# A four-layer graph network on one core: reciprocals brought to the free axis through HBM scratch tensors

## The chip, the cores and the metric

The kernel runs on one core of one Trainium2 chip. A core has five engines with instruction streams of their own: TensorE (matrix products, PE in the profile; PEld is its weight load), VectorE (DVE), ScalarE (ACT), GpSimd (POOL) and SyncE (SP, which here issues every transfer), and 16 DMA engines that move data between HBM and the on-chip memory SBUF. Matmul results land in PSUM banks. Each engine works its stream in order and waits on semaphores for the others. The metric is device time in microseconds (us), as the median of several runs.

## The reference, cut to what matters

The input is 32 independent graphs of 512 nodes, each with a feature matrix x (512 x 256) and a 0/1 adjacency matrix (512 x 512). Four layers follow; each ends in x = layernorm(x + layer(x)).

```
layer 0   attention with 8 heads, scores masked by adj, softmax over the keys:
          out = (softmax(q k^T / sqrt(32), masked) v) Wo + bo
layer 1   relu(((1+eps) x + adj x) W1 + b1) W2 + b2                 hidden 512
layer 2   h = (eps x + adj x) W1 + b1                               hidden 1024
          h = h * rsqrt(mean(h*h over the 1024) + 1e-6) * weight    (an RMS norm)
          silu(h) W2 + b2
layer 3   softplus of a normalised-Laplacian layer
```

Two factors matter here. In layer 0 each node and head has the reciprocal of its softmax sum. In layer 2 each node has one RMS factor. All is computed in float32.

## The kernel before, in words

A graph's 512 nodes are NT = 4 tiles of 128. Activations that feed a product are kept with the features on the partitions and the nodes on the free axis (qT, kT, oT, hT, aT, gT); those that are normalised per node are kept the other way (y, r1, r2). A factor per node is computed with the nodes on the partitions. Where the tensor that it multiplies has the nodes on the free axis (oT and gT), the factor has to be turned and spread over 128 partitions. That is the place of this change.

**Layer 0.** `attend` (called for two groups of four heads) makes, per node tile, a group of four score products with 32 rows each (sc, L776, row-tiled), then on VectorE mask and row minimum (L800), on ScalarE the exponential with its row sums in rs (L814), on VectorE a block transpose (L850), then a store to HBM (via, four DMAs, L862) and a load (pT, L874) that finish the transposition. The value products (po_att, L893, column-tiled) run over two tiles at once, and their result goes unnormalised to oT. `normalise` (L946) then takes reciprocals of all 32 sums per node (L952), `split` (L910) writes each as three bfloat16 parts, TensorE transposes them (pm_t, L934), a copy brings them to SBUF (mT), and eight small matmuls with a constant selection matrix (pr_r, L963) spread them to the 128 partitions in PSUM. VectorE multiplies oT by that (L974). `pair_sum` with wo (po, L991) follows.

**Layer 2.** Eight products with w21 (pg, L1187) give gT; squares on ScalarE (L1263) are summed on GpSimd into ssq (L549). A transpose (L1270), a reduction (L1273) and one small matmul (pm, L1281) bring the sums to the node axis; VectorE finishes the mean (L1295, L1303), GpSimd takes the power -1/2 (rr). Then `split` again (L917, L924, pm_t, mT), four selection matmuls (pb, L1314), and eight VectorE products of gT by weight and factor (L1326), silu in two halves on ScalarE (L1341) and the product with w22 (po, L991).

**The order.** Nothing is scheduled by a compiler: the function `graph` records every operation of every graph with its reads, writes, engine, estimated cost and stage. The class `Order` then plays through all of them: at each step it takes, on the engine that is free first, the operation with the smallest key. The key is graph number times PERIOD plus the operation's due time, which comes from the operation's earliest and latest time in a lone graph (weighted by LATE) plus an offset per stage (LEAD). So three graphs or so are in flight at once, and attention of one is woven into the later layers of another. The instructions are emitted in that order, and each engine keeps it. TURN_DUE is a penalty for changing between row-, column- and untiled matmuls; HASTE moves the last graph forward. Buffers rotate by tag: four PSUM banks with the tag "m" serve nearly all products, the scores have a set of four banks of their own; adjT has two buffers, gT one.

All DMAs of the program are issued in order by SP. A DMA whose input isn't ready blocks those behind it.

Of the kernel before, what the change touches and what calls it, by code (L numbers as in the profile page):

```python
# [9 lines left out]
F32 = mybir.dt.float32  # L10
BF16 = mybir.dt.bfloat16
AF = mybir.ActivationFunctionType
# [7 lines left out]
RMS_EPS = 1e-6  # L20
HEADS = 8

PERIOD = 65998
LEAD = {
    "adjT": 17900, "agg1": -34100, "agg2": -112800, "degree": 46800, "diag": 80200,
    "lap": -5300, "ln0": -81400, "ln1": -47100, "ln2": 88600, "ln3": -37200, "load": -92700,
    "move": 7000, "pv": 8000, "pz": 22200, "qk": 5800, "rinv": -8800, "rms": -91800,
    "scores": -5600, "silu": 57000, "softplus": -39900, "v": -32400, "w11": -49700,
    "w12": -36000, "w21": 10500, "w22": -22500, "wo": 21900, "x3T": -21500, "xT": 67600,
}  # L30


# [27 lines left out]
class Order:  # L60
# [9 lines left out]
    TABLE, TABLE_DUE = 1300, 9000  # L70

    TURN = {"whole": 93, "row": 290, "col": 150}
    TURN_DUE = 500
    LATE = 0.09
    HASTE = 137

    def __init__(self):
        self.ops = []
# [204 lines left out]
def kernel(  # L283
# [51 lines left out]
    nhalf = const.tile([P, NT], F32, name="nhalf")  # L335
    nc.vector.memset(nhalf, -0.5)

    ident_b = const.tile([P, P], BF16, name="ident_b")
    nc.vector.tensor_copy(ident_b, ident)

    def selector(n, wide, name):

        of = const.tile([P, n], F32, name=f"{name}_of")
        nc.vector.tensor_reduce(
            of, ident[:, 0 : 3 * n].rearrange("p (r x) -> p x r", r=3), axis=AX.X, op=ALU.add
        )
        sel = const.tile([P, n, wide], BF16, name=name)  # L350
        nc.vector.tensor_copy(sel, of.unsqueeze(2).to_broadcast([P, n, wide]))
        return sel

    NX = 2 * NT * HPG
    sel_r = selector(NX, HD, "sel_r")
    sel_t = selector(NT, P, "sel_t")


    id_as = ident.rearrange("p (a s) -> p a s", a=4)
# [148 lines left out]
    def graph(b):  # L508
# [10 lines left out]
        def tmp(shape, tag, bufs, name=None, dtype=F32):  # L519
            return Buf(sb, shape, dtype, tag, f"{name or tag}_{b}", bufs)  # L520

        def pe(cost, fn, r, w, *hold, turn="whole"):

            op([("PE", cost, fn, {"turn": turn})], r, w, hold)

        def dve(cost, fn, r, w, port=False):
            op([("DVE", cost, fn, {"port": 1} if port else {})], r, w)
# [41 lines left out]
        def small(name, bufs=2, shape=None):  # L569
            return Buf(sb, shape or [P, NT], F32, "s_" + name, f"{name}_{b}", bufs)  # L570
# [336 lines left out]
            stage[0] = "rinv"  # L907
            evacuate(lambda: oT[:, g, :], po, [(po,)], [(oT, g)])

        def split(src, n, name):  # L910

            parts = tmp([P, 3, n], "p_" + name, 2, name + "p", dtype=BF16)
            left, left_k = src, []
            for r in range(3):
                dve(
                    190,
                    lambda r=r, left=left: nc.vector.tensor_copy(parts[:, r, :], left()),  # L917
                    [(left,)], [(parts, r)], port=True,
                )
                if r < 2:  # L920
                    rest = small(name + "rest", 2, [P, n])
                    dve(
                        180,
                        lambda r=r, left=left, rest=rest: nc.vector.tensor_tensor(  # L924
                            rest(), left(), parts[:, r, :], ALU.subtract
                        ),
                        [(left,), (parts, r)], [(rest,)], port=True,
                    )
                    left = rest
            pm_t = Buf(ps, [P, P], BF16, "m", f"pm_t_{b}", 4)  # L930
            mT = tmp([P, P], "mT_" + name, 1, dtype=BF16)
            pe(
                65,
                lambda: nc.tensor.transpose(  # L934
                    pm_t[0 : 3 * n, :], parts().rearrange("p r x -> p (r x)"), ident_b
                ),
                [(parts, r) for r in range(3)], [(pm_t,)], mT,
            )
            either(
                [(pm_t,)], [(mT,)],  # L940
                (220, lambda: nc.vector.tensor_copy(mT[0 : 3 * n], pm_t[0 : 3 * n, :])),
                (330, lambda: nc.scalar.copy(mT[0 : 3 * n], pm_t[0 : 3 * n, :])),
            )
            return mT

        def normalise():  # L946

            stage[0] = "rinv"
            rv = small("rv", 2, [P, NX])
            dve(  # L950
                240,
                lambda: nc.vector.reciprocal(rv(), rs().rearrange("p g t j -> p (g t j)")),  # L952
                [(rs, g, t, j) for g in range(2) for t in range(NT) for j in range(HPG)],
                [(rv,)],
            )
            mT = split(rv, NX, "sums")
            for g in range(2):
                pr_r = bank("pr_r")

                def spread(g=g, pr_r=pr_r):  # L960
                    for t in range(NT):
                        x = (g * NT + t) * HPG
                        nc.tensor.matmul(  # L963
                            pr_r[:, t * P : (t + 1) * P],
                            lhsT=sel_r[0 : 3 * NX, x : x + HPG].rearrange("p j e -> p (j e)"),
                            rhs=mT[0 : 3 * NX],
                            start=True,
                            stop=True,
                        )

                pe(240, spread, [(mT,)], [(pr_r,)])
                dve(
                    700,
                    lambda g=g, pr_r=pr_r: nc.vector.tensor_tensor(  # L974
                        oT[:, g, :], pr_r(), oT[:, g, :], ALU.mult
                    ),
                    [(pr_r,)], [(oT, g)],
                )

        def pair_sum(lhs, lhs_k, w, w_k, nk, y, step):  # L980
# [156 lines left out]
        x1 = y  # L1137


        def residual(xin, bias_r, bias_k):  # L1140
            r = tmp([P, NT, D], "y", 3)
            pool(
                2400,
                lambda: nc.gpsimd.tensor_tensor(r(), xin(), rows(bias_r), ALU.add),
                [(xin, t) for t in range(NT)] + [(bias_k,)], [(r, t) for t in range(NT)],
            )
            return r

# [49 lines left out]
        stage[0] = "agg1"  # L1198
        set_diagonal(self1, "self1")
        hT = aggregate(x1)  # L1200
        r1 = residual(x1, b12_r, "b12_r")
        set_diagonal(self2, "self2")
        stage[0] = "w11"
        aT = tmp([P, C1, N], "aT", 1)
# [101 lines left out]
        rr = small("rr")  # L1306
        rsqrt(rr, ms, [(ms,)], [(rr,)])

        mT = split(rr, NT, "rms")
        pb = bank("pb")  # L1310

        def spread_rms():
            for t in range(NT):
                nc.tensor.matmul(  # L1314
                    pb[:, t * P : (t + 1) * P],
                    lhsT=sel_t[0 : 3 * NT, t],
                    rhs=mT[0 : 3 * NT],
                    start=True,
                    stop=True,
                )  # L1320

        pe(240, spread_rms, [(mT,)], [(pb,)])
        for m in range(C2):
            dve(
                750,
# [176 lines left out]
        for rt in row_tiles:  # L1502
# [6 lines left out]
            s_ = lambda part=part: sp[:, part]  # L1509
            z_ = lambda part=part: zy[:, part, 0:D]  # L1510
            x_ = lambda part=part: x3[:, part]
            act(cost, lambda s_=s_, z_=z_: nc.scalar.activation(s_(), z_(), AF.Abs), z0, spk)
            act(
                cost,
                lambda s_=s_: nc.scalar.activation(s_(), s_(), AF.Exp, scale=-1.0), [], spk,
# [75 lines left out]
```

## Time and profile before

| What | Before |
|---|---|
| median of 3 runs | 3356.13 us (3354.51 to 3359.38) |
| profiled execution | 3356.19 us |
| span of its trace | 3354.4 us |
| TensorE busy | 3305.2 us |
| VectorE busy | 2823.6 us |
| ScalarE busy | 1887.3 us |
| GpSimd busy | 843.4 us |
| mean share of the 16 DMA engines | 77%, 677.23 MB moved |
| granted TensorE clock | 0.996 |

The span is the time from the first to the last instruction of the profiled execution; the execution itself is 1.8 us longer. Busy time is the union of an engine's instructions. Consecutive matmuls overlap in the trace, since each record lasts until the result is out, so the price of a matmul is best read from the distance between starts. A float32 product appears as two passes.

### The profile page before, as it was taken

To read this page: it belongs to the slowest core of one execution; us is meant where nothing else is said; L and a number is where in the kernel's file an instruction comes from. 1 tells how busy PE (TensorE), PEld (TensorE's weight loads), DVE (VectorE), ACT (ScalarE), POOL (GpSimd) and SP (SyncE) were. 2 spreads that over 40 slices of the span, in tenths; PEclk is the share of its full clock that TensorE was granted. 3 is DMA by queue.
4 is the path that set the end of the run, shared out by engine and by line. 5 is a ranking of instruction groups with operands and counts; after the bars stand their busy time and mean duration, and the time that the engine had idled before them with its cause. 6 is when DMAs were issued, how large, how long until landed. Compare 5 with 4: busy or idle time off the path is not lost.

```text
span 3354.4 us, 55143 instructions
## 1 busy us (share of the span) xinstructions
PE 3305.2 (99%) x19624; PEld 1980.2 (59%) x19624; DVE 2823.6 (84%) x6412; ACT 1887.3 (56%) x3863; POOL 843.4 (25%) x610
## 2 busy tenths in 40 slices
PE   8999999999999999999999999999999999999997
PEld 5556655566565566565666655665655665556654
DVE  7878888888888888888888888888888888888855
ACT  6555565565655655655555655555656556556533
POOL 1222222322222322222222223222222222232221
PEclk9999999999999999999999999999999999999999
DMA  5878878778878787787787787787887887877820
GB/s 143 246 235 216 207 200 222 226 202 211 204 202 234 204 220 197 206 219 226 201 215 207 202 228 214 208 210 201 215 232 199 214 206 201 225 224 183 206 53 13
DMA packets 768195, 677.23 MB, mean 202 GB/s; under 512 B 540208, under 2 KB 592304, under 8 KB 736176
## 3 DMA queue, kind: packets, MB, share of 16 engines
q1 hardware_dynamic: 767920, 673.71, 76.5%
q8 instruction: 155, 2.54, 0.3%
q14 instruction: 120, 0.98, 0.1%
HBM read 380.52 MB, written 293.08 MB: 201 GB/s over the span
## 4 chain that ended last, share of the span: by engine, by line
PE 96%; DVE 1%; ACT 1%; DMA 1%; issue 0%; POOL 0%; SPq 0%; POOLq 0%; DVEq 0%; ACTq 0%
PE po L991 23%; PE ph L1170 13%; PE pg L1187 13%; PE sc L776 8%; PE po_att L893 7%; PE pz L1436 7%; PE pa_l L1478 7%; PE pa L1187 7%; PE pq L703 6%; PE pv L744 3%; ACT pq L814 0%; PE pr_r L963 0%; PE pb L1314 0%; DVE pq L800 0%; DMA via<-pq 0%
## 5 line engine op out<-in xcount | busy, mean ns | idle before, releaser
L814 ACT ACTIVATE pq<-pq,mx 128x512 f32<-128x512 f32 x1024 | 729.0, 714 | 333.3 <-DVE mx L800 265.7
L800 DVE CUSTOM_DVE_ANT_0 pq<-sc,bias 128x512 f32<-128x512 f32 x1024 | 664.3, 685 | 42.3 <-PE sc L776 23.7
L850 DVE STREAM_TRANSPOSE pq<-pq 128x2048 f32<-128x2048 f32 x248 | 567.9, 2296 | 6.4 <-ACT pq L814 6.4
L1187 PE MATMUL pg<-hT,w 128*128 128x512 f32 x1024 | 480.3, 603 | 2.0 <-DVE gT L1242 2.0
L991 PE MATMUL po<-w,gT 128*128 128x256 f32 x2048 | 451.3, 381 | 6.3 <-ACT gT L1341 6.3
L991 PEld LDWEIGHTS po<-w,gT 128*128 128x128 f32 x2048 | 391.3, 191 | 62.1 <-ACT gT L1341 7.1
L549 POOL TENSOR_TENSOR ssq<-ssq,sq 128x512 f32<-128x512 f32 x217 | 276.9, 1276 | 521.6 <-ACT sq L1263 521.2
L1187 PEld LDWEIGHTS pg<-hT,w 128*128 128x128 f32 x1024 | 184.6, 190 | 251.0 <-issue 238.1
L776 PE MATMUL sc<-kT,qT 32*128 32x512 f32 x2048 | 291.9, 640 | 3.0 <-DVE mx L800 3.0
L893 PEld LDWEIGHTS po_att<-pT,v 128*32 128x32 f32 x8192 | 216.3, 110 | 99.1 <-issue 49.2
L893 PE MATMUL po_att<-pT,v 128*32 128x128 f32 x8192 | 251.2, 275 | 5.5 <-DMA pT<-via 5.5
L1478 PE MATMUL pa_l<-zy,adjT 128*128 128x256 f32 x1024 | 243.0, 385 | 0.0
L1044 POOL TENSOR_TENSOR rstd<-ve,nhalf 128x4 f32<-128x4 f32 (+1 forms) x132 | 135.6, 1028 | 422.5 <-DVE ve L1039 417.5
L1242 DVE TENSOR_SCALAR gT<-pg,b_c 128x512 f32<-128x512 f32 x187 | 140.3, 751 | 120.0 <-PE pg L1187 119.9
L549 POOL TENSOR_TENSOR sp<-sp,y 128x1024 f32<-128x1024 f32 x31 | 73.4, 2367 | 657.7 <-ACT sp L1528 644.7
L1436 PE MATMUL pz<-wsn,xnT 128*128 128x512 f32 x512 | 236.9, 606 | 0.7 <-ACT sq L1263 0.6
L1170 PE MATMUL ph<-adjT,y 128*128 128x512 f32 x512 | 227.0, 596 | 4.7 <-ACT y L1070 4.7
L1170 PE MATMUL ph<-adjT,y_att 128*128 128x512 f32 x512 | 228.2, 598 | 0.0
L1187 PE MATMUL pa<-hT,w 128*128 128x512 f32 x512 | 228.1, 598 | 0.0
L991 PE MATMUL po<-w,aT 128*128 128x256 f32 x1024 | 226.5, 379 | 0.0
L991 PEld LDWEIGHTS po<-w,aT 128*128 128x128 f32 x1024 | 194.3, 190 | 28.0 <-ACT aT L1218 0.8
L1478 PEld LDWEIGHTS pa_l<-zy,adjT 128*128 128x128 f32 x1024 | 189.3, 190 | 29.9 <-issue 0.7
(165 smaller groups left out, 4896.3 us busy)
## 6 DMA issues: line engine op xcount, KB each, us to landing
via<-pq SPq DMA_DIRECT2D x992, 256.0 KB, 4.4
pT<-via SPq DMA_DIRECT2D x248, 1024.0 KB, 6.4
adj<-in_adj_dram SPq DMA_DIRECT2D x32, 1024.0 KB, 7.9
adjT<-in_adj_dram SPq DMA_DIRECT2D x124, 256.0 KB, 6.0
x<-in_x_dram SPq DMA_DIRECT2D x32, 512.0 KB, 6.1
xT<-in_x_dram SPq DMA_DIRECT2D x124, 128.0 KB, 5.9
x3d<-y SPq DMA_DIRECT2D x31, 512.0 KB, 3.9
xnT<-x3d SPq DMA_DIRECT2D x124, 128.0 KB, 3.7
```

The costliest lines, as they stand in the source:

```text
L549: lambda: nc.gpsimd.tensor_tensor(dst(), dst(), src(), ALU.add), {},
L703: nc.tensor.matmul(pq(), lhsT=w[:, c, m * P : (m + 1) * P], rhs=xT[:, c, :], start=(c == 0), stop=(c == DC - 1),)
L776: nc.tensor.matmul(sc[:, j, :], lhsT=qT[hp, g, t * P : (t + 1) * P], rhs=kT[hp, g, :], start=True, stop=True,)
L800: lambda t=t, j=j, sc=sc, row=row: nc.vector.tensor_tensor_reduce(out=row(), in0=sc[:, j, :].rearrange("p (a n) -> p a n", a=4), in1=bias[ ...
L814: lambda t=t, j=j, row=row: nc.scalar.activation(row(), row(), AF.Exp, bias=mx[:, t, j : j + 1], scale=-1.0, accum_out=rs[:, g, t, j : j + 1],
L850: lambda pq=pq: nc.vector.transpose(pq().rearrange("p a j c s -> p (a j c s)"), pq().rearrange("p a j c s -> p (a j c s)"),),
L893: nc.tensor.matmul(po[j * HD : (j + 1) * HD, t * P : (t + 1) * P], lhsT=v[:, c, h * HD : (h + 1) * HD], rhs=pT[:, :, j, c, :], start=(c == 0),
L991: nc.tensor.matmul(po[:, i * D : (i + 1) * D], lhsT=lhs[:, k, t * P : (t + 1) * P], rhs=w[:, k, :], start=(i == 0 and k == 0), stop=(i == ...
L1170: nc.tensor.matmul(ph(), lhsT=xin[:, m, c * P : (c + 1) * P], rhs=adjT[:, m, :], start=(m == 0), stop=(m == NT - 1),)
L1187: nc.tensor.matmul(pa(), lhsT=w[:, c, m * P : (m + 1) * P], rhs=hT[:, c, :], start=(c == 0), stop=(c == DC - 1),)
L1436: nc.tensor.matmul(pz(), lhsT=xnT[:, c, t * P : (t + 1) * P], rhs=wsn[:, c, :], start=(c == 0), stop=(c == DC - 1),)
L1478: nc.tensor.matmul(pa[:, i * D : (i + 1) * D], lhsT=adjT[:, m, t * P : (t + 1) * P], rhs=zy[:, m, D : 2 * D], start=(m == 0), stop=(m == N ...
```

## The change

The turning by TensorE is replaced, in both places, by a round trip through scratch tensors in HBM, with a read that repeats a row over partitions.

In `normalise`, VectorE takes the reciprocals and transposes the 128 x 32 tile in 32 x 32 blocks. Four DMAs store the blocks in rd, which then holds one row of 128 nodes for each tile and head; four DMAs read the rows back, each repeated over the 32 partitions of its head, to the SBUF tensor of. VectorE multiplies oT by of.

In layer 2, one DMA stores the 512 factors, element by element, as a row of HBM (rrd), and one reads this row into all 128 partitions (pb, which is now an SBUF tensor with the tag of the squares). `split`, its casts and transposes, the selection matmuls and their constants go.

The planner's constants are new: PERIOD, all 28 LEAD offsets, TURN_DUE, LATE and HASTE. So the order of all operations differs between the two kernels. Two operations also get a dependency that only the planner sees: the residual of layer 1 of graph b comes after the first softplus operation of graph b-2.

```diff
-PERIOD = 65998
+PERIOD = 62758
 LEAD = {
-    "adjT": 17900, "agg1": -34100, "agg2": -112800, "degree": 46800, "diag": 80200,
...
+    "adjT": 30100, "agg1": -27200, "agg2": -109700, "degree": 60800, "diag": 115000,
...
-    TURN_DUE = 500
-    LATE = 0.09
-    HASTE = 137
+    TURN_DUE = 1750
+    LATE = 0.50
+    HASTE = 2161
...
-        def split(src, n, name):
...
         def normalise():
             rv = small("rv", 2, [P, NX])
+            def turned():
+                nc.vector.reciprocal(rv(), rs().rearrange("p g t j -> p (g t j)"))
+                nc.vector.transpose(rv(), rv())
...
-            mT = split(rv, NX, "sums")
+            rd = Buf(dr, [NX, P], F32, "rd", f"rd_{b}", 2)
+            of = tmp([P, 2, NT, P], "of", 1)
+            def away():
+                for i in range(4):
+                    nc.sync.dma_start(
+                        rd[:, 32 * i : 32 * i + 32], rv[32 * i : 32 * i + 32, :]
+                    )
+            def back():
+                v = rd().rearrange("(gt j) q -> j gt q", j=HPG)
+                for j in range(HPG):
+                    nc.sync.dma_start(
+                        of[j * HD : (j + 1) * HD].rearrange("p g t q -> p (g t) q"),
+                        v[j].partition_broadcast(HD),
+                    )
...
-                pe(240, spread, [(mT,)], [(pr_r,)])
                 dve(
                     700,
-                    lambda g=g, pr_r=pr_r: nc.vector.tensor_tensor(
-                        oT[:, g, :], pr_r(), oT[:, g, :], ALU.mult
-                    ),
-                    [(pr_r,)], [(oT, g)],
+                    lambda g=g: nc.vector.tensor_tensor(
+                        oT[:, g, :], of[:, g].rearrange("p t q -> p (t q)"), oT[:, g, :], ALU.mult
+                    ),
+                    [(of,)], [(oT, g)], port=True,
                 )
...
-        mT = split(rr, NT, "rms")
-        pb = bank("pb")
...
-        pe(240, spread_rms, [(mT,)], [(pb,)])
+        rrd = Buf(dr, [NT, P], F32, "rrd", f"rrd_{b}", 2)
+        pb = tmp([P, N], "sq", 2, "pb")
+        def rr_away():
+            with nc.allow_non_contiguous_dma(reason="one factor per node"):
+                nc.sync.dma_start(rrd().rearrange("t p -> p t"), rr())
+        op([("SP", 3000, rr_away, {"issue": 560, "lat": 300})], [(rr,)], [(rrd,)])
+        op(
+            [(
+                "SP", 4500,
+                lambda: nc.sync.dma_start(
+                    pb(), rrd().rearrange("t p -> (t p)").partition_broadcast(P)
+                ),
+                {"issue": 560, "lat": 300},
+            )],
+            [(rrd,)], [(pb,)],
+        )
```

## The prediction

> **What bounds the kernel now.** I read the page first: busy time and the chain that ended last. Then TensorE's waits, busy time by stretch, and TensorE's timeline in one graph.
>
> ```profile
> span 3354.4 us, 55143 instructions
> PE 3305.2 (99%) x19624; PEld 1980.2 (59%) x19624; DVE 2823.6 (84%) x6412; ACT 1887.3 (56%) x3863; POOL 843.4 (25%) x610
> PE 96%; DVE 1%; ACT 1%; DMA 1%; issue 0%; POOL 0%; SPq 0%; POOLq 0%; DVEq 0%; ACTq 0%
> ```
>
> The second answer, for a stretch in the middle (second number: TensorE's busy time, fourth: VectorE's):
>
> ```profile
> core 0: us, PE busy (x) PEld busy (x) DVE busy (x) ACT busy (x) POOL busy (x), PEclk, DMA share, GB/s
> 1000.00:2000.00 1000.00, 1000.00 (x5980) 593.91 (x5979) 862.14 (x1956) 570.65 (x1178) 263.94 (x189) 1.00 0.80 213
> ```
>
> TensorE never idles there. A busy matmul could still be a slow one, so I looked at starts. The one-column matmul pm comes at 1586.08 and next at 1688.21: 102.13 us a graph, the same to 0.01 us over 28 graphs in a row. TensorE's waits list nothing between 300 and 3150 us; the 30 us that it does wait lie in the first and last graphs. So in 28 of 32 graphs the time is TensorE's instruction list, and I price that list by starts, since durations overlap:
>
> ```profile
> 1586.08 0.29 PE L1281 MATMUL pm<-red,quad 128*128 128x16 f32 x2
> 1586.22 1.96 PE L1436 MATMUL pz<-wsn,xnT 128*128 128x512 f32 x4
> 1588.11 1.14 PE L776 MATMUL sc<-kT,qT 32*128 32x512 f32 x8
> ...
> 1590.15 1.89 PE L1478 MATMUL pa_l<-zy,adjT 128*128 128x256 f32 x8
> 1591.97 0.22 PE L934 MATMUL pm_t<-ident_b,rmsp 128*12 128x128 bf16 x1
> 1592.12 1.99 PE L1478 MATMUL pa_l<-zy,adjT 128*128 128x256 f32 x8
> 1594.05 0.39 PE L1314 MATMUL pb<-mT_rms,sel_t 12*128 12x128 bf16 x4
> 1594.37 3.72 PE L1478 MATMUL pa_l<-zy,adjT 128*128 128x256 f32 x16
> 1598.02 1.14 PE L776 MATMUL sc<-kT,qT 32*128 32x512 f32 x8
> ...
> 1601.79 13.98 PE L991 MATMUL po<-w,gT 128*128 128x256 f32 x64
> 1615.69 1.14 PE L776 MATMUL sc<-kT,qT 32*128 32x512 f32 x8
> ```
>
> ```profile
> 1655.85 1.88 PE L703 MATMUL pq<-xT,wk 128*128 128x512 f32 x4
> 1657.57 0.22 PE L934 MATMUL pm_t<-ident_b,sumsp 128*96 128x128 bf16 x1
> 1657.62 1.94 PE L1187 MATMUL pg<-hT,w 128*128 128x512 f32 x4
> 1659.39 0.61 PE L963 MATMUL pr_r<-mT_sums,sel_r 96*128 96x128 bf16 x8
> 1659.94 1.14 PE L776 MATMUL sc<-kT,qT 32*128 32x512 f32 x8
> ```
>
> A pass of 512 columns takes (1657.57-1655.85)/4 = 0.43 us, one of 256 about 13.90/64 = 0.216. Before a row-tiled group (sc) about 0.09 us are lost, after it 0.10.
>
> **What the Trainium skill says.** (1) "TensorEngine Tiling (Array Packing)", Key Properties: a change of tiling mode drains TensorE. The trace agrees, and shows it for the narrow matmuls pm_t (12 columns of weights) and pb (12 rows) too. (2) The Trainium skill, "DMA: Bandwidth & Descriptors", "Anatomy of one DMA" (written for another issuing path): a fixed part of some 2 us, mostly the receipt of the write. The trace's smallest medians to landing are 3.0 to 3.9 us, so I use the trace. (3) The Trainium skill, "SBUF — State Buffer", "SBUF: two separate sides": a VectorE operation with two SBUF inputs and a GpSimd one exclude each other. Agrees: L1152 (two SBUF inputs) takes 654/693/1936 ns min/median/max, L974 with one input from PSUM 677/683/693.
>
> **The change, part by part.**
> *TensorE, sums.* One pm_t, 0.05; eight pr_r, 0.55 less the 0.09 that any matmul would lose ahead of sc: 0.46. Together 0.51 x 32 = 16.3 us.
> *TensorE, RMS.* pa_l, pm_t and pb stand from 1590.15 to 1598.02 = 7.87; 32 passes of 0.216 are 6.91, and 0.09 ahead of sc stays: 0.87 goes. In the 30 graphs with this pattern 26.1 us.
> *Moved order.* Constants of the planner change with it (PERIOD, LEAD and three more), so TensorE's whole order is new. In the built order pm stands right ahead of an sc group in 29 graphs, where a drain is paid anyway; now it costs 0.14 and (1.89-4x0.43-0.09) = 0.08 after it, of which I take 0.17 off: 4.9 us. Visits to row or column mode fall from 295 to 289, 6 x 0.2 = 1.2 us. All other matmuls are the same in number.
> Sum 48.5 us: the period becomes about 100.6.
> *VectorE* loses ten small casts and subtractions and two copies, 66 us in all by its groups, and gains 32 transposes of 128x32. It had 16% idle: nothing by itself. The two oT products and eight gT products now have both inputs in SBUF. GpSimd has nothing queued during the gT products; oT products stand between its ssq additions and can lose one of them (1.28 us), with over 5 us to the next sc.
> *DMA.* Per graph 10 more issues on SP's queue (56 before), 4 of 4 KB, 4 of 128 KB, one of 2 KB in 4-byte elements and one of 256 KB. SP's issues in the trace run 0.3 to 0.7 us: 3 to 7 us of 102, on a queue that spends most of its time waiting. About 0.8 MB on top of 21 MB.
> *Sums' round trip.* The reciprocals are ready when the last exponential is; the second po_att evacuation comes more than 30 us later in the built order, and the wo product later still. Two transfers of some 4 us, with via and pT issues between, are covered.
> *RMS round trip*, the tight one. Between ms and the first gT product VectorE's built order holds four half-statistics (2x0.53), four zy (0.67), four score tiles (0.61), a transposition (2.22) and one y_att (0.60): 9.0 us, stretched to 9.8 by the pz passes it follows. The power on GpSimd takes 1.1 of it: 8.7 remain for both transfers. Not shown in the trace: a store of 512 4-byte elements and a read of one row into 128 partitions. Nearest rows: xnT (1024 runs of 128 B) 3.7, x3d 3.9, via 4.4; the column loads at the start 3.8 to 9.0. I take 2 x 4.0 = 8; bounds 6 and 14. Beyond VectorE's cover, TensorE asks for the first pa_l bank only some 3 us later, and SP, blocked at the broadcast, holds back three xT loads and a pT that TensorE needs with some 3 us to spare. So TensorE stalls from 11.7 us of round trip on.
> *Ends.* In the last graph only 8.8 us of TensorE work lie between pm and the w22 product (4 pz and 32 pa_l passes). The chain is 1.8 (ms, power) + 8 + 2.6 (4 gT) + 2.0 (silu) = 14.4: a stall of about 5.6 in place of 1.56 now, +4. In the one before, 10.4 lie there: 4 in place of 4.77, about -1. First graphs: the 5.5 us wait for pT may shrink or not: 0. Sum +3.
> *Total.* 3354.4-48.5+3 = 3309; for small unseen waits in a new order I add 1.5; the profiled time lies 1.8 above its span: 3312. The median of the runs (3356.1) is that of the profiled run (3356.2), so no further shift.
>
> **Rivals.**
> *A, TensorE stays full:* 3312, own range 3301 to 3324. For it: the built order keeps 18 us between pm and w22 in the steady graphs, against the chain's 14.4.
> *B, VectorE becomes the bound in two stretches.* From the arrival of adjT (its buffer is released by pa_l, then SP issues four loads, 5.4 us in the timeline, and 6.0 to land) through two transposes, ACT's copies, statistics and the diagonal there are about 19 us of chain, and the order has 18.8 us of matmuls between pa_l and the next ph (20.5 before). Then qT and aT evacuations free PSUM banks with 0 to 1 us to spare. 0.3 to 1.2 us a graph: 3321 to 3348. Against it: VectorE's work falls by 2 us a graph.
> *C, slower: the RMS round trip is late.* Above 11.7 us each microsecond costs 30. The gain of about 44 is gone at 13.2 us: two transfers of 6.6, as slow as the median pT (6.4, but that moves 1 MB). At 14 us 3381. For it: 4-byte elements, 80% DMA share. Against: tiny payloads.
> *D, the change doesn't do what it says:* the matmuls might only hide idle time of TensorE. The 1000 of 1000 us speak against it; this would give 3356.
>
> **Numbers.** A 0.56, B 0.26, C 0.12, D or a mishap of the new order that just cancels 0.06. The runs before spread by 0.15%, so 0.2%, 6.7 us, is about what can be told from no change. Faster: A, B and a little of D, 0.83; same 0.05; slower 0.12. The range runs from A's lower end, 3300, to where C begins, 3357.
>
> **What would show it.** Right: pm to pm 100.6 us in the middle graphs, pm_t, pr_r and pb gone, TensorE busy 1000 of 1000 still; the transfers to rrd and pb about 4 us each; a longer wait of po for silu in the last graph. B would show as waits of ph for the diagonal or of pa and po for VectorE, repeated some 30 times. C would show VectorE idle ahead of the gT products on a DMA, and po or po_att waiting every graph. The forecast is wrong if small stores land in more than 6 us, or if the new order starves TensorE somewhere I haven't priced.

## The result: 15% slower, and the profile after

The changed kernel took 3867.47 us (median of four runs, 3855.66 to 3870.0) against 3355.56 for the kernel before beside it: a ratio of 1.1516, 95% interval 1.1491 to 1.1542. The forecast was 3312. Its page (span, and busy time of each engine) and its busy time in the middle of the run read:

```profile
span 3853.9 us, 54292 instructions
PE 3424.6 (89%) x19176; PEld 2029.3 (53%) x19176; DVE 2774.7 (72%) x6056; ACT 1888.6 (49%) x3866; POOL 842.9 (22%) x610
```

```profile
core 0: us, PE busy (x) PEld busy (x) DVE busy (x) ACT busy (x) POOL busy (x), PEclk, DMA share, GB/s
1000.00:2000.00 1000.00, 896.17 (x5020) 533.02 (x5009) 738.11 (x1600) 498.46 (x1013) 225.44 (x161) 0.95 0.74 190
```

TensorE has 448 matmuls fewer, as forecast, and yet 119 us more of busy time, and it stands still for 10% of the middle, where it never did before. The granted clock (PEclk) is 0.95 for 1.00. From pm to pm a graph takes 118.0 us in the median of the middle graphs, for 102.13 before and the forecast 100.6.

TensorE's waits, with total, count and longest, name the places:

```profile
PE po_att L875 <- DMA pT<-via: 142.4, 28, 7.7
PE sc L758 <- DVE mx L782: 124.0, 56, 9.9
PE pz L1401 <- DVE xnT L1386: 44.2, 27, 3.6
```

The first and the third come about once a graph, the second about twice. One graph of TensorE's timeline shows all three; it begins with the stretch that the prediction showed of the kernel before:

```profile
1694.47 1.98 PE L1401 MATMUL pz<-wsn,xnT 128*128 128x512 f32 x4 [1.26 <-DVE xnT L1386]
1696.30 0.35 PE L1242 MATMUL pm<-red,quad 128*128 128x16 f32 x2
1696.95 1.14 PE L758 MATMUL sc<-kT,qT 32*128 32x512 f32 x8 [0.30 <-DVE mx L782]
...
1705.25 7.17 PE L1443 MATMUL pa_l<-zy,adjT 128*128 128x256 f32 x32
...
1720.32 1.94 PE L875 MATMUL po_att<-pT,v 128*32 128x128 f32 x32 [5.81 <-DMA pT<-via]
1722.19 15.59 PE L952 MATMUL po<-w,gT 128*128 128x256 f32 x64
...
1773.73 2.09 PE L758 MATMUL sc<-kT,qT 32*128 32x512 f32 x8 [3.57 <-DVE mx L782]
1775.75 9.17 PE L1131 MATMUL ph<-adjT,y 128*128 128x512 f32 x16
```

The pa_l passes run without a break now: by starts 32 of them take 7.11 us (1705.25 to 1712.36), for 7.87 with pm_t and pb among them. But three waits (1.26, 5.81, 3.57) follow, and the work after a wait is slow: 64 po passes take 15.59 us for 13.98 before, an sc group 2.09 for 1.14. Windows at the two longer waits show why (columns as in the window above; the third number from the end is the granted clock):

```profile
1718.50:1725.00 6.50, 4.68 (x39) 3.65 (x40) 4.42 (x14) 4.06 (x5) 1.01 (x1) 0.50 1.03 251
1725.50:1738.00 12.50, 12.50 (x61) 10.75 (x64) 11.03 (x17) 11.69 (x21) 4.74 (x2) 1.00 0.85 212
1773.10:1779.50 6.40, 5.76 (x13) 2.23 (x14) 5.36 (x14) 5.35 (x16) 2.35 (x1) 0.50 0.09 35
1780.00:1785.00 5.00, 5.00 (x16) 2.05 (x18) 2.87 (x3) 0.62 (x2) 0.00 (x0) 1.00 0.69 154
```

The waits begin at 1714.51 and 1770.16, 5.81 and 3.57 us long. Before each is over the clock falls to 0.50, and it comes back to 1.00 only some 5 to 6 us after the work has begun again. The Trainium skill, "TensorE: Matmul & The Clock Gate", Part 1, says that an idle window of about 3.4 us halves TensorE's clock until it has been busy for about as long, and that these windows run freely. The trace agrees in the halving; the half clock lasts longer here than one such window, some 6.5 us in each case.

The transfers, in the trace's list of DMA issues (KB each, median us from issue to landing):

```profile
of<-rd SPq DMA_DIRECT2D x128, 128.0 KB, 8.3
x3d<-y SPq DMA_DIRECT2D x31, 512.0 KB, 10.9
xnT<-x3d SPq DMA_DIRECT2D x124, 128.0 KB, 7.2
pb<-rrd SPq DMA_DIRECT2D x32, 256.0 KB, 5.2
rd<-rv SPq DMA_DIRECT2D x128, 4.0 KB, 1.8
rrd<-rr SPq DMA_DIRECT2D x32, 2.0 KB, 10.0
```

The smallest of the new ones is the slowest: 2 KB in 10.0 us. Also x3d and xnT, which the change doesn't touch, take 10.9 and 7.2 us for 3.9 and 3.7. SP's timeline and VectorE's show what the round trip of the RMS factors does in the graph above:

```profile
1698.82 0.39 SPq L1275 DMA_DIRECT2D rrd<-rr  x1
1707.72 0.34 SPq L1281 DMA_DIRECT2D pb<-rrd  x1
1708.16 5.06 SPq L571 DMA_DIRECT2D xT<-in_x_dram  x3
1713.39 0.54 SPq L856 DMA_DIRECT2D pT<-via  x1
```

```profile
1706.67 0.65 DVE L966 TENSOR_TENSOR y_att<-po,y_att 128x512 f32<-128x512 f32 x1
1713.49 2.74 DVE L1291 SCALAR_TENSOR_TENSOR gT<-gT,rw_c,pb 128x512 f32<-128x512 f32 x4 [6.17 <-DMA pb<-rrd]
...
1766.60 0.69 DVE L935 TENSOR_TENSOR oT<-of,oT 128x512 f32<-128x512 f32 x1 [7.18 <-DMA of<-rd]
```

SP issues the store at 1698.82 and stands at the broadcast until it has landed, 8.9 us later; the three xT loads and the pT that TensorE lacks at 1714.51 stand behind it. VectorE waits 6.17 us for pb, and 7.18 us later on for of.

### The profile page after: what moved, and what is told of

Read it like the earlier page. It is cut to its first block, busy times and chain, and to the rows that moved or that the text cites. A ratio compares the mean times of both kernels' runs of the same rounds, so it can differ in the third digit from the quotient of the medians.

```text
span 3853.9 us, 54292 instructions
## 1 busy us (share of the span) xinstructions
PE 3424.6 (89%) x19176; PEld 2029.3 (53%) x19176; DVE 2774.7 (72%) x6056; ACT 1888.6 (49%) x3866; POOL 842.9 (22%) x610
## 2 busy tenths in 40 slices
DMA packets 830655, 702.94 MB, mean 182 GB/s; under 512 B 565808, under 2 KB 650672, under 8 KB 798640
## 5 line engine op out<-in xcount | busy, mean ns | idle before, releaser
L952 PE MATMUL po<-w,gT 128*128 128x256 f32 x2048 | 490.4, 403 | 23.8 <-ACT gT L1306 22.3
L952 PEld LDWEIGHTS po<-w,gT 128*128 128x128 f32 x2048 | 414.5, 204 | 100.4 <-ACT gT L1306 23.8
L1148 PE MATMUL pg<-hT,w 128*128 128x512 f32 x1024 | 463.4, 601 | 1.1 <-DVE hT L523 1.1
L875 PE MATMUL po_att<-pT,v 128*32 128x128 f32 x8192 | 283.2, 293 | 169.7 <-DMA pT<-via 142.4
L758 PE MATMUL sc<-kT,qT 32*128 32x512 f32 x2048 | 312.3, 680 | 124.5 <-DVE mx L782 124.0
L875 PEld LDWEIGHTS po_att<-pT,v 128*32 128x32 f32 x8192 | 233.1, 117 | 265.7 <-DMA pT<-via 150.8
L1291 DVE SCALAR_TENSOR_TENSOR gT<-gT,rw_c,pb 128x512 f32<-128x512 f32 x256 | 172.4, 746 | 164.8 <-DMA pb<-rrd 164.8
L1306 ACT ACTIVATE gT<-gT 128x2048 f32<-128x2048 f32 x64 | 122.3, 1911 | 324.1 <-DVE gT L1291 324.1
L1131 PE MATMUL ph<-adjT,y 128*128 128x512 f32 x512 | 272.5, 692 | 5.8 <-DVE y L1023 3.1
L1443 PE MATMUL pa_l<-zy,adjT 128*128 128x256 f32 x1024 | 232.2, 384 | 8.2 <-DVE zy L1412 8.2
## 6 DMA issues: line engine op xcount, KB each, us to landing
x3d<-y SPq DMA_DIRECT2D x31, 512.0 KB, 10.9
```

What stands on the lines that cost most here:

```text
L758: nc.tensor.matmul(sc[:, j, :], lhsT=qT[hp, g, t * P : (t + 1) * P], rhs=kT[hp, g, :], start=True, stop=True,)
L875: nc.tensor.matmul(po[j * HD : (j + 1) * HD, t * P : (t + 1) * P], lhsT=v[:, c, h * HD : (h + 1) * HD], rhs=pT[:, :, j, c, :], start=(c == 0),
L952: nc.tensor.matmul(po[:, i * D : (i + 1) * D], lhsT=lhs[:, k, t * P : (t + 1) * P], rhs=w[:, k, :], start=(i == 0 and k == 0), stop=(i == ...
L1131: nc.tensor.matmul(ph(), lhsT=xin[:, m, c * P : (c + 1) * P], rhs=adjT[:, m, :], start=(m == 0), stop=(m == NT - 1),)
L1148: nc.tensor.matmul(pa(), lhsT=w[:, c, m * P : (m + 1) * P], rhs=hT[:, c, :], start=(c == 0), stop=(c == DC - 1),)
L1291: lambda m=m: nc.vector.scalar_tensor_tensor(out=gT[:, m, :], in0=gT[:, m, :], scalar=rw_c[:, m : m + 1], in1=pb(), op0=ALU.mult, op1=ALU. ...
```

## The experiments

Four theories were set against each other. 1: the RMS round trip is longer than its cover (the prediction's rival C). 2: the sums' round trip, which the prediction held to be covered, stops VectorE. 3: the new order has stalls of its own, whatever the transfers take. 4: the added bytes and issues crowd out the others. After e1 and e4 a theory 1b was added: the store of single elements harms the transfers that are issued behind it. Times are medians, ratios to the kernel before on the same chip:

| run | us | ratio, 95% interval |
|---|---|---|
| e1 pb doesn't wait for the store | 3779.1 | 1.126, 1.121 to 1.131 |
| e5 as e1, no store to rrd | 3634.3 | 1.083, 1.077 to 1.088 |
| e6 as e5, oT waits for nothing | 3459.2 | 1.031, 1.028 to 1.034 |
| e7 no new transfer at all | 3444.7 | 1.026, 1.023 to 1.029 |
| e2 oT alone waits for nothing | 3647.5 | 1.087, 1.082 to 1.091 |
| e3 e1 and e2 together | 3622.1 | 1.079, 1.076 to 1.083 |
| e4 block store | 3538.1 | 1.054, 1.051 to 1.057 |
| e16 e4 with the 4-byte store (e9: 3682.9) | 3704.0 | 1.104, 1.101 to 1.107 |
| e10 e4, oT waits for nothing | 3371.4 | 1.004, 1.003 to 1.006 |
| e15 e1, store on another queue | 3771.1 | 1.123, 1.121 to 1.125 |
| e18 e1, elements 512 bytes apart | 3645.5 | 1.086, 1.081 to 1.092 |
| e8 planner told | 3892.5 | 1.160, 1.156 to 1.163 |
| e11 retuned, a | 3318.6 | 0.989, 0.987 to 0.990 |
| e12 retuned, b | 3334.7 | 0.994, 0.992 to 0.995 |
| e13 before, retuned | 3342.5 | 0.995, 0.994 to 0.997 |
| e17 e11 with the 4-byte store (e14: 3584.4) | 3578.1 | 1.066, 1.063 to 1.069 |

**Taking the waits away, one by one (e1, e2, e3).** The planner's keys stay as they are, so the planned order is that of the changed kernel; only what is read differs.

```diff
 # e1
-    pb(), rrd().rearrange("t p -> (t p)").partition_broadcast(P)
+    pb(), x[b].rearrange("n d -> (n d)")[0:N].partition_broadcast(P)
 # e2 (e3 is both)
-    oT[:, g, :], of[:, g].rearrange("p t q -> p (t q)"), oT[:, g, :], ALU.mult
+    oT[:, g, :].rearrange("p (a d) -> p a d", d=D),
+    bo_r.unsqueeze(1).to_broadcast([P, 2, D]),
+    oT[:, g, :].rearrange("p (a d) -> p a d", d=D), ALU.mult
```

> The changed kernel, but the broadcast into pb reads a row of the input instead of rrd, so nothing waits for the store of the RMS factors, which is still made. Left out: gT is multiplied by numbers that aren't the factors. Theory 1 (the RMS round trip delays VectorE's gT products, and the store's 10 us block SP's queue so that pT comes late for po_att): the waits of gT for pb (5.7 us a graph) and of po_att for pT (5.1) are gone, and TensorE keeps its full clock through the w22 product; 30 x (5.8 + 1.6 + about 0.6) = 240 us less, about 3625. Theory 2 (the sums' round trip holds VectorE) alone: no more than 30 us less. Theory 3 (the order from the new constants is at fault, whatever the transfers take): about 3860, the waits turn up elsewhere. Theory 4 (the DMA engines are too full): about 3860, since every transfer is still made.

> The changed kernel, but the two oT products multiply by a constant row instead of of, so nothing waits for the sums' round trip, which is still made. Left out: oT isn't divided by the softmax sums. Theory 2: the wait of oT for of (7.2 us a graph) goes, and with it the wait of sc for VectorE (3.6), the slow sc (2.1 for 1.1 us) and the slow ph (9.2 for 7.1): 30 x 6.6 = 200 us less, about 3670. Theory 1 alone: no more than 30 us less. Theories 3 and 4: about 3860.

> Both of the last two edits: all transfers are made, nothing of the arithmetic waits for them. Left out: the division by the sums and the RMS factors. Theories 1 and 2 together: the gains add up, 240 + 200, about 3430; if the clock drops too were all due to these waits, down to the predicted 3312. Theory 3: over 3550, since an order that is bad in itself stays bad. Theory 4: over 3700.

Theory 2 holds in its size: 220 us less for the forecast 200. Theory 1 as written does not: freeing pb from the store gave 88 us, not 240. In e1 po_att still waited for pT, 90.6 us in all, and gT for pb, 90.2 us: the broadcast is issued right behind the store, and landed after 12.8 us in the median. Both edits together left 3622, where theory 3 had said "over 3550". So something besides the two waits was at work.

**Leaving the transfers out (e5, e6, e7),** in the same planned order.

```diff
 # e5: e1 and
-    nc.sync.dma_start(rrd().rearrange("t p -> p t"), rr())
+    pass
 # e6: e5 and e2.  e7: e6, and rd, of and pb aren't transferred either;
-    in1=pb(),
+    in1=bo_r.unsqueeze(1).to_broadcast([P, 2, D]),
```

> The first experiment's kernel (pb read from the input) with the store to rrd left out as well: what is still there of the RMS round trip is one broadcast read. Left out: the RMS factors. Theory 1b, formed on the first and the fourth run (the 4-byte store does its harm in the DMA queue: the transfers issued behind it, xT and pT first, land late, so freeing pb alone brought 3860 only to 3779): the waits of po_att for pT go, 3540 to 3600, near the 3538 of the block store. Theory 1 in its first form (the harm is the waiting of SP and VectorE, which the first experiment had already taken away): no change against 3779.

> The same, and the oT products multiply by a constant row, so that nothing waits for the sums' round trip either; its transfers are made. Left out: the RMS factors and the division by the sums. Theories 1b and 2: the 200 us of the sums' round trip come off on top, 3340 to 3400. Theory 3 (the order is bad in itself): over 3450.

> The changed kernel's order of work with none of its four new transfers: gT and oT are multiplied by a constant row. Left out: the RMS factors and the division by the sums. This is what the sum of the prediction priced, TensorE's list without a stall: 3309 by that sum, 3305 to 3330 with small waits. Theory 3: the new order has stalls of its own, over 3400. Theory 4 (the added bytes and issues crowd out x3d, xnT and adj): this one is lower by more than 30 us than the one before it.

Leaving out a store of 2 KB a graph for which nothing waits is worth 145 us (3779 to 3634). With the store gone, po_att's waits for pT fall from 90.6 to 7.6 us. Then 175 us go with the wait for of, and only 14 with all the transfers left: theory 4 is not the cause. x3d and xnT still land in 7.1 us each in e7, for 3.9 and 3.7 before: that much of their delay is the order's. e5 and e6 ended 34 and 59 us above what theories 1b and 2 allowed, and e7 shows why: at 3445 the order is on its own, and it is 89 us slower than the kernel before with 448 matmuls fewer: theory 3 is right as well. Two of its waits are seen in e7's TensorE waits. For the first, SP's timeline follows, of e7 and then of the kernel before:

```profile
PE pz L1393 <- DVE xnT L1378: 43.8, 28, 3.6
PE ph L1125 <- issue: 36.1, 24, 2.4
```

```profile
1939.23 1.05 SPq L856 DMA_DIRECT2D pT<-via  x1
1941.20 7.24 SPq L571 DMA_DIRECT2D xnT<-x3d  x4
```

```profile
1570.91 2.72 SPq L589 DMA_DIRECT2D xnT<-x3d  x4
```

In e7 the four xnT loads stand right behind a pT of 1 MB; their issue alone takes 7.24 us, and pz, due at 1951.05, waits 1.53 us for them. In the order before they start just as far ahead of pz (9.9 us), but no pT stands right before them and they are issued in 2.72 us.

For ph the list names no releaser ("issue"), but VectorE's timeline and TensorE's do:

```profile
1885.66 0.68 DVE L1107 TENSOR_TENSOR adjT<-diag,self 128x512 f32<-128x512 f32 x1
```

```profile
1886.55 1.96 PE L1125 MATMUL ph<-adjT,y_att 128*128 128x512 f32 x4 [1.07 <-issue]
```

VectorE's addition of the diagonal to adjT, which ph reads, ends at 1886.34, and ph starts 0.21 us later. It is so in all 24 of these waits, with 0.21 us each time. This is the sign that the prediction named for its rival B, waits of ph for the diagonal. Here the four adjT loads begin when pa_l has ended (1866.31) and take 6.99 us to issue, VectorE waits 2.04 us for them, and from 1866.31 to ph there are 20.2 us of chain for 19.2 of matmuls.

**The store's form (e4, e9, e16).** A 32x32 block transpose puts the factors of a block in four rows:

```diff
-        rr = small("rr")
-        rsqrt(rr, ms, [(ms,)], [(rr,)])
+        rrw = small("rrw", 2, [P, 32])
+        dve(60, lambda: nc.vector.memset(rrw(), 0.0), [], [(rrw,)])
+        rsqrt(lambda: rrw[:, 0:NT], ms, [(ms,)], [(rrw,)])
 ...
+        dve(100, lambda: nc.vector.transpose(rrw(), rrw()), [], [(rrw,)])
 ...
-            nc.sync.dma_start(rrd().rearrange("t p -> p t"), rr())
+            for a in range(4):
+                nc.sync.dma_start(rrd[:, 32 * a : 32 * a + 32], rrw[32 * a : 32 * a + NT, :])
```

> The changed kernel, whole in what it computes; the RMS factors are turned by a 32x32 block transpose on VectorE and stored in 4 DMAs of 4 runs of 128 bytes each in place of 512 elements of 4 bytes. Theory 1 in its form that the time of the store comes from its 4-byte elements: the store lands in about 2 to 3 us, the chain from the power to pb takes 9 instead of 15.5 us, the wait of gT falls to under 1.5 us and that of po_att goes: 180 to 240 us less, 3625 to 3690. If the store is slow for another reason (the queue, the load of the engines): 8 to 10 us still, about 3860.

e9 and e16 put the store of single elements back into e4's order:

```diff
-            for a in range(4):
-                nc.sync.dma_start(rrd[:, 32 * a : 32 * a + 32], rrw[32 * a : 32 * a + NT, :])
+            nc.sync.dma_start(rrd().rearrange("t p -> p t"), rrw[:, 0:NT])
 # e9: the transpose goes to columns that nobody reads; e16: to a tile of its own, and
+        rrw.tile_bufs = 4
```

> The block-store kernel in its own order, with one thing put back: the factors are stored as 512 elements of 4 bytes (the block transpose is still made, into columns that nobody reads). The first eight runs compared kernels whose order or data also changed; this one changes the store alone. Theory 1b (the 4-byte store costs by its own round trip of some 15 instead of 7 us and by what it holds back in the queue): 150 to 300 us above the block store's 3538, 3690 to 3840. If the better time of the block store came from its other order instead: within 30 us of 3538.

> e9 once more without a wait of its own making: in e9 VectorE's clearing of the factors' tile two graphs on waited 136 us for the slow store. Here that tile has four buffers in place of two, and the unused transpose goes to a tile of its own; the order is the block-store kernel's. Theory 1b: most of e9's loss stays, since gT then waits for pb where the clearing had waited: 3640 to 3690. If e9's loss was mainly that wait: 3540 to 3590.

The block store gained 329 us, more than expected, since its added instructions also changed the planned order. In the fixed order the store's form is worth 166 us (3704 to 3538). e9 had a wait of its own (the clearing of rrw); taking it out made no gain, so e9's 145 us were the store's too. (e9 ended 7 us below the range expected of it, e16 14 us above.) e4's SP timeline shows 2.9 us from the store to the broadcast, for 8.9:

```profile
1680.99 1.27 SPq L1278 DMA_DIRECT2D rrd<-rrw  x4
1683.90 0.34 SPq L1286 DMA_DIRECT2D pb<-rrd  x1
```

**How the store harms what doesn't wait for it (e15, e18).**

```diff
 # e15: e1 and
-    nc.sync.dma_start(rrd().rearrange("t p -> p t"), rr())
+    nc.scalar.dma_start(rrd().rearrange("t p -> p t"), rr())
 # e18: e1 and
-    rrd = Buf(dr, [NT, P], F32, "rrd", f"rrd_{b}", 2)
+    rrd = Buf(dr, [NT, P, P], F32, "rrd", f"rrd_{b}", 2)
-    nc.sync.dma_start(rrd().rearrange("t p -> p t"), rr())
+    nc.sync.dma_start(rrd[:, :, 0].rearrange("t p -> p t"), rr())
```

> The first experiment's kernel (3779; pb read from the input, the 4-byte store still made and nothing waiting for it), with the store issued on ScalarE's DMA queue instead of SP's. Left out: the RMS factors. If the store harms the transfers behind it because they stand in the same queue: near the 3634 of the kernel without the store, 3620 to 3670. If it harms them by holding the DMA engines that all queues share: 3740 to 3790.

> The first experiment's kernel (3779; pb read from the input, nothing waits for the 4-byte store), with each of the 512 elements stored 512 bytes from the next in a larger rrd in place of side by side. Left out: the RMS factors. If the store is slow because neighbouring elements share a line in HBM and are read, changed and written one after another: near the 3634 without the store, 3620 to 3680. If each small element costs by itself: 3750 to 3800.

Another queue changes next to nothing (3771), so the harm isn't the place in SP's queue. That fits the Trainium skill, "DMA: Bandwidth & Descriptors", "Issuing engines are not separate DMA queues". (ScalarE isn't what slows e15 in its stead: in nearly all graphs its next operation starts 0.6 us after it has issued the store, and waited for VectorE and not for the store.) Spacing the elements 512 bytes apart takes 134 of the 145 us away with the same 512 elements at the same place in the queue. The two traces count the same 830,655 packets, 16,896 more than e5's. SP also waits for the factors before the store in both (206.7 and 205.8 us in all), so that wait, which e5 leaves out along with the store, isn't the cause either. The lists of DMA issues show the difference, first e1, then e18:

```profile
pb<-in_x_dram SPq DMA_DIRECT2D x32, 256.0 KB, 12.8
```

```profile
pb<-in_x_dram SPq DMA_DIRECT2D x32, 256.0 KB, 3.9
rrd<-rr SPq DMA_DIRECT2D x32, 2.0 KB, 2.1
```

Spaced apart, the store lands in 2.1 us, for 10.0 in the changed kernel, and the broadcast behind it in 3.9 for 12.8. So it is the neighbourhood of the elements that costs, not their number. The same page's Specifications say that a transfer below 512 bytes is a read-modify-write. The single elements of both forms and the 128-byte runs of e4 are all below; only the form that puts 128 elements into each 512 bytes is slow here. That writes which share such a piece of memory wait for each other is a likely reading; the runs show the spacing, not the mechanism. The SP timelines of e1 and e18, each from the store on:

```profile
1790.07 0.38 SPq L1275 DMA_DIRECT2D rrd<-rr  x1
...
1794.72 5.64 SPq L571 DMA_DIRECT2D xT<-in_x_dram  x3
1800.53 2.33 SPq L856 DMA_DIRECT2D pT<-via  x1
```

```profile
1730.55 0.38 SPq L1275 DMA_DIRECT2D rrd<-rr  x1
...
1735.60 2.02 SPq L571 DMA_DIRECT2D xT<-in_x_dram  x3
1737.78 1.90 SPq L856 DMA_DIRECT2D pT<-via  x1
```

Nothing in e1 makes SP wait for the store, but the next loads take 5.64 us to issue for 2.02, and pT is 10.5 us behind the store for 7.2. In the changed kernel the DMA engines move almost nothing meanwhile (windows of before, during and after the store):

```profile
1690.00:1698.80 8.80, 7.24 (x31) 4.28 (x31) 6.46 (x19) 3.16 (x9) 2.29 (x2) 1.00 0.95 267
1698.80:1707.70 8.90, 8.90 (x86) 5.58 (x85) 7.91 (x14) 6.11 (x13) 0.00 (x0) 1.00 0.06 4
1707.70:1713.40 5.70, 5.70 (x30) 4.12 (x29) 0.00 (x0) 0.00 (x0) 0.00 (x0) 1.00 0.31 76
```

A share of 0.06 and 4 GB/s: the 10 us are no queueing behind other traffic.

**The sums' round trip (e10),** e4 with the edit of e2.

> The block-store kernel, but the oT products multiply by a constant row and so don't wait for the sums' round trip, whose transfers are still made. Left out: the division by the sums. Theory 2: sc waits 94 us for VectorE in the block-store kernel because of it, and the two slow stretches after it add as much again; 100 to 170 us off 3538, 3370 to 3440. What then remains above the 3309 of the prediction's sum is the order's own (theory 3 gave 136 us of this in the changed kernel's order). If the waits for of are harmless here: over 3500.

3371, at the lower edge: the wait for of is worth 167 us here. This kernel makes all the transfers, and its busy time in the middle shows TensorE full again (columns as in the same stretch of the changed kernel):

```profile
1000.00:2000.00 1000.00, 999.82 (x5902) 598.66 (x5899) 849.89 (x1874) 588.73 (x1200) 261.15 (x187) 1.00 0.84 222
```

Its period is 100.91 us, 0.3 above the forecast 100.6. It still doesn't beat the kernel before, because its ends are long: the first two periods take 133.7 and 114.8 us for 111.8 and 102.1, the last three and the rest after pm some 10 us more. That is about 45 us, against 32 gained at 1.22 us a graph in the middle 26.

**Telling the planner (e8), and choosing its constants anew (e11, e12, e13).**

```diff
 # e8
-    op([("SP", 3000, rr_away, {"issue": 560, "lat": 300})], [(rr,)], [(rrd,)])
+    op([("SP", 10000, rr_away, {"issue": 560, "lat": 300})], [(rr,)], [(rrd,)])
-    "SP", 4500,
+    "SP", 5500,
-    [("SP", 5800, back, {"issue": 2240, "lat": 300})],
+    [("SP", 10000, back, {"issue": 3200, "lat": 300})],
```

> The changed kernel, whole in what it computes, with the planner told what the trace shows of the new transfers: 10 us in place of 3 for the store of the factors, 5.5 in place of 4.5 for pb, 10 in place of 5.8 for the reads of of. If the planner's wrong durations are the root, it puts other work between and the waits of oT and gT shrink: 3450 to 3600. By theory 1b it can't mend what the store does to the transfers behind it: the waits for pT stay, and 3650 to 3850 is what is left.

Both expectations failed: 3892, slower than the changed kernel. pT is hardly waited for any more (14.7 us in all), but xnT is, for 98.8 us, and w22 for its gT, 95.0. Truer durations under constants chosen for others only move the stalls.

e11 and e12 are e4 with the last line of that diff and new constants. e11's are below; e12 has another set; e13 is the kernel before with new constants of its own.

```diff
-PERIOD = 62758
+PERIOD = 67211
 LEAD = {
-    ... "rinv": -47500, "rms": -69600, ... "x3T": -22400, ...
+    ... "rinv": -4404200, "rms": -3372300, ... "x3T": -2916700, ...
-    TURN_DUE = 1750
-    LATE = 0.50
-    HASTE = 2161
+    TURN_DUE = 2418
+    LATE = 0.08
+    HASTE = 440.6
```

In words: the two round trips and the x3d transfers go as soon as they can, whatever else is due.

> Whole in what it computes: the change with the block store, the planner told 10 us for the reads of of, and its constants (PERIOD, LEAD, TURN_DUE, LATE, HASTE) chosen anew by a replay of the planned order in which transfers queue one behind another and the granted clock drops after a stall, with amounts taken from the traces of these runs. That replay puts before at 3387 to 3456, the changed kernel at 3671 to 3865, and this one at 3340 to 3393. If the loss was the two round trips and the order around them, and not the change itself: 3290 to 3350, below before. If moving the factors by HBM can't be hidden at all: over 3400.

> The same with another set of constants, at 3348 to 3386 in the replay: 3290 to 3350 if the change can be hidden, over 3400 if not.

> The kernel before with constants chosen anew by the same replay (which puts it at 3350 to 3379; with its own constants at 3387 to 3456). It is the control for the two retuned kernels. Its TensorE was busy without a gap in 28 of 32 graphs at 102.13 us each, so there only the ends and the number of mode changes can give: 3325 to 3356. If it falls to 3319 as well, the retuned kernel's gain is the re-tuning and not the change; if it stays above 3335, most of that gain is the change's.

e11 takes 3318.55 us, 1.1% below the kernel before (interval 0.987 to 0.990). Its page (busy time, and the chain that ended last):

```profile
PE 3270.4 (99%) x19176; PEld 1953.1 (59%) x19176; DVE 2709.3 (82%) x5979; ACT 1953.0 (59%) x4005; POOL 839.9 (25%) x610
PE 96%; DVE 1%; DMA 1%; ACT 1%; SPq 0%; issue 0%; POOLq 0%; POOL 0%; DVEq 0%
```

The middle graphs take 101.10 us, and the longest wait of TensorE in the whole run is 5.7 us, once. The control e13 comes to 3342.47 with 101.95 us a graph. Each against the kernel before beside it, e13 gained 15.6 us and e11 38.6. So the retuning by itself gave some 15 us; the other 23 fit the change with its block store, since 0.85 us x 26 graphs = 22 of it are seen in the middle, where TensorE is full in both. How near either set of constants is to its best isn't known; e12, with the same operations, lies 16 us above e11 and only 8 below e13, though its middle graphs take 101.20 us, nearly as e11's.

**The 4-byte store in a good order (e14, e17):** e11 with the edits of e9 and e16.

> The faster retuned kernel in its own order, with the factors stored as 512 elements of 4 bytes again (the block transpose is made into columns that nobody reads). Theory 1b: the store alone undoes the gain, 3420 to 3520. If a good order could have hidden the store: below 3356.

> The same mending of e14 (where the clearing waited 159 us), in the faster retuned kernel's order. Theory 1b: the 4-byte store alone still undoes the gain, 3450 to 3580. If a good order hides it: below 3356.

e14 came out above its range; e17, without the wait of its own, 6 us lower, so here too that wait had only stood in for another. The store alone costs e11's order 260 us (3318.6 to 3578.1), 8.2 us a graph (109.3 for 101.10). e17's waits of VectorE and of TensorE:

```profile
DVE gT L1320 <- DMA pb<-rrd: 217.9, 32, 8.1
...
PE po L977 <- DVE zy L1483: 186.4, 29, 7.4
```

VectorE waits 6.8 us a graph for pb. The zy additions stand behind that in its queue, and the next w22 product (po) waits 6.4 us for them in 29 graphs.

## Why the prediction was wrong, step by step

From 3312 to 3867 there are 555 us. Taken away in the order e1, e5, e6, e7 they part into 88 (pb's wait for the store), 145 (the store's effect on the transfers behind it, pb's own broadcast among them), 175 (waiting for of), 14 (the new transfers' mere presence) and 133 (3445 to 3312, the order's own). The shares depend on the sequence: the wait for of is worth 220 when it goes first, and both waits together (245) are worth less than the sum of each by itself (88 and 220).

- *TensorE, sums, RMS and moved order (16.3, 26.1, 6.1 us):* right in size where nothing else stands in the way. The sum gave a period of 100.6; e10 has 100.91 and e11 101.10. Their orders visit row or column mode 315 and 346 times for the 289 of the changed order; an estimate at the prediction's 0.2 us a visit makes the sum 100.8 and 101.0 for them. The term for the moved order belongs to the changed order, which never ran full, and isn't tested.
- *RMS round trip, "I take 2 x 4.0 = 8; bounds 6 and 14":* this step failed. From the end of the power to the first gT product the changed kernel takes 14.5 us in the median (13.7 to 20.1): 9.1 from the store to the broadcast's issue and 5.3 from there to gT. The broadcast landed in 5.2, not far from its price; the store was priced as one more small transfer and landed in 10.0. The price came from the lower rows of its list (xnT 3.7, x3d 3.9); the column loads in the same list, which are made of single elements as the store is, had taken up to 9.0. In 128-byte runs the store did take under 3 (e4).
- *The cover, 8.7 us, and the queue behind the broadcast:* right. 14.5 less 8.7 is 5.8, and VectorE waited 6.17; SP held pT back, and TensorE waited 5.81 for it. The 3 us that TensorE was to have in hand were gone: the three xT loads ahead of pT took 5.06 us to issue behind the store, for 2.02 in e18.
- *Rival C, "each microsecond costs 30":* the right mechanism with too small a price. At 14.5 us it gives 3312 + 2.8 x 30 = 3396. The pb wait and the store cost 233 us in the changed order, 166 and 260 in two others. Two things were not in the price: the store holds up transfers that don't wait for it, and a stall of TensorE is followed by a stretch at a lower clock. The second can be read from e7: the same order and the same 19176 matmuls, 3295.9 us busy in e7 and 3424.6 in the changed kernel, so about 129 of the 407 us between their spans are slower passes and the other 278 are standing still.
- *Sums' round trip, "covered":* this step failed too. It looked at the last user, the wo product and the second evacuation of po_att, more than 30 us off. The first oT product needs only the first evacuation, and the planner, which took 5.8 us for the reads of of, put it early in VectorE's queue. rd is issued at 1748.90, the reads of of from 1756.63 behind via and pT, and the product starts at 1766.60, 7.18 us after VectorE was ready for it; the exponents' row maxima and with them sc stand behind it.
- *"For small unseen waits in a new order I add 1.5":* mis-sized. The order without any new transfer is 133 us above the forecast: waits at pz (43.8 us) for xnT loads that stand right behind a pT in SP's queue, waits at ph (36.1) for the diagonal, and longer ends (below). e10, whose order the same constants made for the block store, has hardly any of these waits at pz and ph: they belong to the order and not to the change.
- *Ends, +3:* mis-sized. In e10's order the first and last graphs take 45 us more, in e7's 22; e11 shows that this belongs to the constants.
- *Rival A* ("the built order keeps 18 us between pm and w22 against the chain's 14.4") rested on the two round trips of 8 us. *Rival B* came true in part: waits of ph for the diagonal appeared, 1.1 us a graph in e7 against its 0.3 to 1.2, with the chain of about 19 us against 18.8 of matmuls that it described. It is a small part of the loss. VectorE as a whole was not the bound: its busy time fell to 72%, and it waited for transfers. *D* fell.
- *Two readings were off without effect on the sum:* "The trace's smallest medians to landing are 3.0 to 3.9 us" passes over the last two stores to the output, 2.1 us; and pm is a matmul of 16 columns, not one.

What stays open: why elements side by side hold up the other transfers.

## What to carry to other kernels

Before a value goes through HBM, look at the pieces that its store writes: turn it first, so that they are longer than one element (128 bytes in e4), and price a store of single elements by a run of its own. When a wait moves to another engine, price it at its first reader in that engine's queue and count what stands behind, not at the last reader. Where a planner's constants were chosen for other operations, the change and the constants need separate experiments: keep the order and take out one transfer at a time.

## What the runs showed of the hardware that was not expected

- A store of 512 elements of 4 bytes, side by side in HBM, lands in 10.0 us with the DMA engines 6% busy, and in 2.1 with the elements 512 bytes apart. From the store to the broadcast that waits for it there are 9.1 us in the median, and 2.9 when it is made of 16 runs of 128 bytes (e4).
- With nothing waiting for it, it costs the kernel 145 us in 32 graphs, 4.5 us each, by what it does to the transfers behind it; on another queue nearly as much (3771 for 3779), and hardly at all with its elements 512 bytes apart (3645, against 3634 without it).
- Waits of 3.6 and 5.8 us bring TensorE's granted clock to 0.50 for some 6.5 us. In the changed kernel's clock record half clock follows on none of TensorE's 42 waits of 0.5 to 1.5 us, on 10 of the 21 of 1.5 to 3 us, and on 60 of the 62 longer ones. Waits of some 1.5 us, two in most graphs, as in e7, leave it at 0.99 in the middle.
